# Layer 2's adjacency polynomial kept as two 64-column graphs below each other, with a new hand-written order of the steps

## The chip, the cores and the metric

The kernel runs on one core of a Trainium2 chip (trn2). The metric is the device time of one execution in microseconds; the kernel before has a median of 2142.81 us over three runs (2142.8 to 2144.53).

## The reference

128 graphs of 64 nodes with 256 features pass four graph layers in fp32; each layer is followed by a residual sum and a layer norm. What bears on this change is layer 2, and the GRU of layer 3 that the kernel runs beside it:

```python
# layer 1: normalised adjacency with self loops
adj = adj + eye(n);  d = adj.sum(-1) ** -0.5
x = layernorm(x + d[:, :, None] * adj * d[:, None, :] @ (x @ W) + b)
# layer 2: K = 4 terms of the row-normalised adjacency An = adj / (row_sum + 1e-9)
curr = h @ W.T;  out = w[0] * curr
for k in (1, 2, 3):
    curr = An @ curr;  out = out + w[k] * curr
x = layernorm(x + leaky_relu(out + b, 0.2))
# layer 3: five rounds of a GRU cell, A01 = (adj != 0)
for l in range(5):
    h = gru(A01.T @ (h @ weight[l]), h)
x = layernorm(x + h * mask)
```

The kernel does not multiply `An` three times with the features. It forms the transposed polynomial `w0 I + w1 An + w2 An^2 + w3 An^3` once for each graph (times the row sums) and gathers the features through it in one product.

## The kernel before

**Tiling.** The 128 graphs are worked on in 16 chunks of 8. A chunk's tile has 128 partitions: two graphs of 64 nodes below each other, and four such pairs side by side (`NP = 4`). A matrix of a pair, such as `Ab` or `AT1`, is a 128 x 128 block-diagonal matrix: the two 64 x 64 graphs on the diagonal and zeros beside it, zeroed once by GpSimd. `aB` holds the same adjacency dense: 128 partitions by 64 columns, two graphs below each other.

**Stages.** Layer 0 comes first (to about 325 us of the profiled span), then a loop of 79 steps for layers 1 to 3, then a tail. In a step one chunk makes one of its five GRU rounds on TensorE while the elementwise part of the other row's last round runs on VectorE, ScalarE and GpSimd. Two rows of chunks alternate, so ten steps (a block) finish two chunks; a step is named here by its number modulo ten.

**The order by hand.** In the loop the order of every engine's instructions is the order in which the program issues them, and that is the string of letters in `ORDERS`: "8", "9", "0", "1" for those steps, "p" for steps 2 to 7. A letter with a number calls one method (`step`, L1126 and on):

- `R1` to `R7` and `N1` to `N7`: the seven products of the gates r and z, and of n. An `R` has 8 matmul instructions in the trace, an `N` has 4 (each fp32 matmul counts as two). Products 1, 4, 6, 7 add up in one PSUM bank (`parz`, `pan`), 2 in another (`pbrz`, `pbn`), 5 and 3 in a third (`pdrz`, `pdn`). The pool `pg` has five banks for the six that a step takes, so a step's later `N5` starts only when an earlier bank, that of `R2`, has been read.
- `r1`, `r6`, `r7`, `n1`, `n6`, `n7`: ScalarE copies the bank (L845); the next product into it waits for that copy.
- `A2`, `A7`, `A3` and `B2`, `B7`, `B3`: VectorE adds bank and copy (L849). `R3` waits for `A7`, and `N3` waits for `B7`, which must have read the third bank. `N5` waits for `A2` in the sense above.
- `S` sigmoid, `T`/`t` tanh (ScalarE), `X` the reset gate (VectorE, L983 and L984), `U`/`u` the state update (VectorE, L946 to L948, three instructions).
- `f0`, `f1` turn the new state by VectorE and store it by a DMA, `d0`, `d1` fetch it back, `l` issues 14 loads of the next chunk, all on SP's queue, which works in order. `e` and `h` are sums on GpSimd (`Th`), `y` turns the state of a chunk that comes next.
- `G`: the messages of the next round, 16 matmuls (`pa`, L254), two ScalarE copies into `agg`, then three sums `Ta` on GpSimd (L805 to L807).
- `p`: one part of the work of layers 1 and 2 for the chunks to come, or of the output of those that are done.

**The parts.** The generator `mid` (L264) does layers 1 and 2 of a chunk in 19 parts, called M1 to M19 here; two chunks follow each other in a block, those of the second with a dash. M1: transpose `aB` into `AT1`, and `A01`. M2: row sums and their roots. M3: `dg` (diagonal of row sums), `poly3` on ScalarE, `An`. M4: add `w3 A` to it. M5: finish `AT1`. M6: first power (`power`, four matmuls, then one VectorE sum). M7: gather `ag1`. M8: bias into `xt`. M9: second power. M10, M11: products with layer 1's weights. M12: norm statistics, M13: the norm applied (four instructions, L185). M14: gather `ag2` of the normalised `xt` through the polynomial. M15 to M17: products with layer 2's weights, ScalarE, sums (L370). M18, M19: statistics and norm. The output of a chunk has four parts, O1 to O4; O4 applies a norm on ScalarE (L182).

`piece` gives the outputs' parts precedence and then goes on in `mid`. Which `p` gets which part is thereby fixed by how many stand in each string and how many of these come after `G` in step 9, where the first output is queued. In the blocks 1 to 6 of before, the first chunk's M3 is the first `p` of step 2, M13 the first of step 4, M18 the first of step 5.

Of the kernel before, what the change touches and what calls it, by code (L numbers as in the profile page):

```python
# [9 lines left out]
F32 = mybir.dt.float32  # L10
AF = mybir.ActivationFunctionType
ALU = mybir.AluOpType
# [3 lines left out]
B, N, D, HID, L = 128, 64, 256, 512, 5  # L16
# [11 lines left out]
NP = CB // 2  # L28
# [13 lines left out]
class Unit:  # L42
# [23 lines left out]

ORDERS = {
    "p": """
h u4 l u3 R1 r1 t7 R2 p u7 R5 f0 f1 e R6 r6 d0 N1 N2 A2 n1 y B2 p N6 R7 S2 X2
r7 n6 T2 p N5 R4 A7 S7 N7 n7 p B7 R3 S4 U2 N4 A3 S3 d1 X7 N3 B3 X3 X4 G p T4 T3  # L70
""",
    "8": """
h u3 u4 R1 f0 R2 p t7 l u7 r1 R5 f1 R6 N1 d0 n1 p p N2 B2 d1 N6 A2 r6 S2 X2 R7
N5 r7 R4 p A7 n6 N7 y R3 e p n7 B7 N4 A3 S4 S7 T2 X7 N3 S3 B3 X4 G X3 T4 p U2
T3
""",
    "9": """
u3 u4 R1 h R5 t7 u7 R2 r1 A2 f0 d0 R6 p f1 l N1 r6 n1 p N2 B2 S2 R7 X2 d1 p N6
r7 N5 n6 T2 R4 A7 N7 S4 e U2 n7 p R3 y B7 S7 N4 X7 G p N3 A3 S3 B3 X4 X3 T4 T3
""",  # L80
    "0": """
u3 h t7 l R1 u4 u7 R2 R5 r1 R6 f0 f1 N1 A2 r6 n1 N2 N6 R7 S2 y B2 N5 d0 p n6 r7
X2 e T2 N7 A7 p U2 d1 n7 R4 S7 p B7 R3 A3 G p N4 N3 S4 X7 S3 B3 X4 X3 T4 T3
""",
    "1": """
p h u4 R1 R2 t7 l u7 r1 u3 A2 f0 f1 R5 R6 N1 e N2 r6 n1 S2 B2 d0 p N6 n6 R7 N5
r7 A7 y N7 n7 X2 d1 T2 p p R4 B7 R3 N4 S7 U2 X7 S4 A3 N3 B3 S3 X3 G X4 p T4 T3
""",
}

# [2 lines left out]
def gnn_stack(  # L93
# [25 lines left out]
    nc = tc.nc  # L119

    wp = ctx.enter_context(tc.tile_pool(name="wp", bufs=1))
    small = ctx.enter_context(tc.tile_pool(name="small", bufs=4))
    keep = ctx.enter_context(tc.tile_pool(name="keep", bufs=1))
# [9 lines left out]
    def spread(src, n, name, pool=wp, eng=None):  # L133

        return const(bass.AP(tensor=src.tensor, offset=src.offset, ap=[[0, 128], [1, n]]), [128, n], name, eng, pool)
# [72 lines left out]
    def psum(name):  # L208
        return pt.tile([128, 512], F32, tag="pt", name=name)
# [50 lines left out]
    state = {}  # L260
    Ab = keep.tile([128, NP, 128], F32, name="Ab")
    AT1 = keep.tile([128, NP, 128], F32, name="AT1")

    def mid(c, first=False):  # L264

        aB = adjs.pop(c)
        A01 = keep.tile([128, NP, 128], F32, name="A01", bufs=4)
        with tc.issue_after(evictions[-1].ins) if first else nullcontext():
            for two in range(2):
                b = slice(two * N, (two + 1) * N)  # L270
                nc.vector.transpose(AT1[b, :, b], aB[b])
        with tc.issue_after(evictions[-1].ins) if first else nullcontext():
            nc.vector.tensor_scalar(A01, Ab, 0.0, None, op0=ALU.not_equal)
        if not first:
            yield
        rsum = small.tile([128, NP], F32, name="rsum")
        with tc.issue_after(evictions[-1].ins) if first else nullcontext():
            nc.vector.tensor_reduce(rsum, Ab, AX.X, ALU.add)
        rdeg = small.tile([128, NP], F32, name="rdeg")
        nc.vector.tensor_scalar(rdeg, rsum, 1.0, None, op0=ALU.add)  # L280
        root = inv_sqrt_begin(rdeg, NP, 128, "d1")
        rinv = small.tile([128, NP], F32, name="rinv")
        nc.vector.tensor_scalar(rinv, rsum, 1e-9, None, op0=ALU.add)
        nc.vector.reciprocal(rinv, rinv)

        nc.vector.tensor_scalar(rsum, rsum, 1e-9, None, op0=ALU.add)
        if not first:
            yield
        dg = keep.tile([128, NP, 128], F32, name="dg", bufs=1)
        nc.vector.tensor_mul(  # L290
            dg, ident[:, None, :].to_broadcast([128, NP, 128]), rsum[:, :, None].to_broadcast([128, NP, 128])
        )
        poly = keep.tile([128, NP, 128], F32, tag="poly", name="poly3", bufs=2)
        nc.scalar.activation(poly, dg, AF.Identity, scale=cw[:, 2:3])
        An = keep.tile([128, NP, 128], F32, name="An", bufs=1)
        nc.vector.tensor_mul(An, Ab, rinv[:, :, None].to_broadcast([128, NP, 128]))
        yield


        dinv1 = inv_sqrt_end(*root)  # L300
        with tc.high_priority():
            nc.vector.scalar_tensor_tensor(poly, AT1, cw[:, 3:4], poly, op0=ALU.mult, op1=ALU.add)
        if not first:
            yield
        nc.vector.tensor_add(AT1, AT1, ident[:, None, :].to_broadcast([128, NP, 128]))
        for two in range(2):
            b = slice(two * N, (two + 1) * N)
            nc.vector.tensor_mul(AT1[b, :, b], AT1[b, :, b], dinv1[b, :, None].to_broadcast([N, NP, N]))
        yield

        def power(poly, k):
            p = psum("pp").rearrange("p (q n) -> p q n", q=NP)
            for q in range(NP):
                nc.tensor.matmul(p[:, q, :], An[:, q, :], poly[:, q, :], start=True, stop=True)  # L314
            poly = keep.tile([128, NP, 128], F32, tag="poly", name=f"poly{k}", bufs=2)
            with tc.high_priority():
                nc.vector.scalar_tensor_tensor(poly, dg, cw[:, k : k + 1], p, op0=ALU.mult, op1=ALU.add)
            return poly

        def product(u, W):  # L320
            p = psum("pd").rearrange("p (q d) -> p q d", q=2)
            for h in range(2):
                q = 2 * u + h
                for k in range(2):
                    nc.tensor.matmul(  # L325
                        p[:, h, :], ag[:, k, q * 128 : (q + 1) * 128], W[:, k, :], start=k == 0, stop=k == 1
                    )
            return p

        xt = xts.pop(c)  # L330
        poly = power(poly, 1)
        if not first:
            yield
        ag = gather(halves(xt), AT1, "ag1")
        if not first:
            yield
        nc.vector.tensor_add(xt, xt, l1bs[:, None, :].to_broadcast([128, NP, D]))
        if not first:
            yield
        poly = power(poly, 0)  # L340
        yield
        for u in range(NP // 2):
            p = product(u, L1W)
            for h in range(2):
                q = 2 * u + h
                nc.vector.scalar_tensor_tensor(
                    xt[:, q, :], p[:, h, :], dinv1[:, q : q + 1], xt[:, q, :], op0=ALU.mult, op1=ALU.add
                )
            if not first:
                yield  # L350
        norm = norm_stats(xt)
        norm = norm_root(*norm)
        yield
        norm_apply(xt, *norm)
        yield


        ag = gather(halves(xt), poly, "ag2")
        yield
        for u in range(NP // 2):  # L360
            p = product(u, L2W)
            v = keep.tile([128, 2, D], F32, name="v", bufs=1)
            for h in range(2):
                q = 2 * u + h
                nc.scalar.activation(
                    v[:, h, :], p[:, h, :], AF.Prelu, bias=cb, scale=rinv[:, q : q + 1], alpha=0.2
                )
            if not first:
                yield
            nc.vector.tensor_add(xt[:, 2 * u : 2 * u + 2, :], v, xt[:, 2 * u : 2 * u + 2, :])  # L370
        if not first:
            yield
        norm = norm_stats(xt)
        norm = norm_root(*norm)
        yield
        norm_apply(xt, *norm)
        state[c] = (xt, A01)
        yield
# [12 lines left out]
    with ExitStack() as c0:  # L391
# [8 lines left out]
        loads, A, AG, HG, S2, Z, XO = {}, {}, {}, {}, {}, {}, {}  # L400
# [209 lines left out]
        p = psum0("pw")  # L610
# [3 lines left out]
        ident = const(c_ident, [128, 128], "ident", nc.scalar)  # L614
# [40 lines left out]
        for i in range(-2, NU + 1):  # L655
# [59 lines left out]
                    nc.vector.tensor_mul(gb2, b2c.rearrange("p (g k) -> p g k", k=2), gw[:, :, None].to_broadcast([128, NG, 2]))  # L715
            elif i == 1:
                with tc.issue_after(powers[-1].ins):
                    for t in (Ab, AT1):
                        nc.gpsimd.memset(t, 0.0)
                    cw = spread(conv_w, 4, "cw", eng=nc.gpsimd)  # L720
                    cb = spread(conv_b, 1, "cb", eng=nc.gpsimd)
                    l1bs = spread(l1b, D, "l1bs", eng=nc.gpsimd)
                    L1W = const_later(l1w.rearrange("(k p) e -> p k e", p=128), [128, 2, D], "L1W")
                    L2W = const_later(l2wT.rearrange("(k p) e -> p k e", p=128), [128, 2, D], "L2W")
                    bih = const_later(bihT, [128, 6], "bih")
                    bhh = const_later(bhhT, [128, 6], "bhh")
                    mask = const_later(maskT, [128, B // 2], "mask")
# [551 lines left out]
```

## Time and profile before

The profiled execution took 2143.39 us, of which 2141.6 us are its span; the granted clock of TensorE was 0.998.

| | busy, us | share of the span | instructions |
|---|---|---|---|
| TensorE matmul (PE) | 2111.7 | 99% | 10738 |
| TensorE weight load (PEld) | 1817.7 | 85% | 10738 |
| VectorE (DVE) | 1667.3 | 78% | 3849 |
| ScalarE (ACT) | 979.4 | 46% | 2006 |
| GpSimd (POOL) | 597.3 | 28% | 635 |

The busy time of TensorE is the union of its matmuls' modelled durations. These overlap: a matmul of 256 columns is shown with 379 ns, and the next one starts 216 ns after it. A gap in the stream is therefore visible only in part as idle time; the distance from start to start shows it in full. The rows that touch the polynomial (mean duration of one):

| line | what | count | ns |
|---|---|---|---|
| L271 DVE | transpose of 64 x 256, one for each half | 32 | 434 |
| L290 DVE | `dg` 128 x 512 | 16 | 768 |
| L294 ACT | `poly3` 128 x 512 | 16 | 722 |
| L302 DVE | `poly3` sum 128 x 512 | 16 | 925 |
| L305 DVE | identity added, 128 x 512 | 16 | 693 |
| L308 DVE | `AT1` scaled, 64 x 256 | 32 | 524 |
| L314 PE | power, 128 columns | 256 | 275 |
| L317 DVE | power's sum from PSUM, 128 x 512 | 32 | 742 |

### The profile page before, as it was taken

What the parts mean: (1) busy time and instruction counts of PE and PEld (TensorE: products, weight loads), DVE (VectorE), ACT (ScalarE), POOL (GpSimd) and SP (SyncE); (2) the same over time, 40 slices, a digit from 0 to 9 for tenths busy, and PEclk for the clock granted to TensorE, in tenths of its full rate; (3) what the DMA queues carried; (4) which work ended last, traced back from release to release, by engine and by line L of the source; (5) the groups of instructions that cost most, each with busy time, mean ns of one, the idle gap of its engine ahead of it and who ended that gap; (6) DMA issues with size and microseconds to landing.
All of it is one profiled execution on the core that took longest, in us unless ns stands there. A gap on an engine that the chain in (4) does not pass through costs nothing.

```text
span 2141.6 us, 31460 instructions
## 1 busy us (share of the span) xinstructions
PE 2111.7 (99%) x10738; PEld 1817.7 (85%) x10738; DVE 1667.3 (78%) x3849; ACT 979.4 (46%) x2006; POOL 597.3 (28%) x635
## 2 busy tenths in 40 slices
PE   9999999999999999999999999999999999999997
PEld 6777788888888888888888888888888888888886
DVE  3345667777888799788979898889888897888766
ACT  3333344444544455444544454444444454445444
POOL 3411131222323323222323232223232232323222
PEclk9999999999999999999999999999999999999999
DMA  6642110223421253114321342224311521234121
GB/s 166 176 134 64 37 39 21 59 55 66 95 67 40 53 110 76 43 46 87 90 52 42 76 96 63 51 62 85 81 40 47 106 74 40 60 62 96 42 59 40
DMA packets 521995, 149.77 MB, mean 70 GB/s; under 512 B 488702, under 2 KB 516860, under 8 KB 521836
## 3 DMA queue, kind: packets, MB, share of 16 engines
q1 hardware_dynamic: 516996, 142.58, 27.7%
q0 software_dynamic: 2128, 4.77, 0.9%
q8 instruction: 85, 1.39, 0.3%
q10 hardware_dynamic: 2712, 0.42, 0.1%
q14 instruction: 74, 0.61, 0.1%
HBM read 82.67 MB, written 65.01 MB: 69 GB/s over the span
## 4 chain that ended last, share of the span: by engine, by line
PE 78%; DVE 15%; issue 2%; DMA 2%; SPq 1%; ACT 1%; POOL 0%; DVEq 0%; POOLq 0%; ACTq 0%
PE parz L825 20%; PE pdrz L825 10%; PE pan L825 10%; PE pa L254 7%; PE pd L325 5%; PE pdn L825 5%; PE pbrz L825 5%; PE ps L516 5%; PE ph L500 4%; PE pbn L825 2%; DVE RZ L947 2%; DVE NI L983 1%; DVE RZ L946 1%; PE pp L314 1%; DVE NI L984 1%
## 5 line engine op out<-in xcount | busy, mean ns | idle before, releaser
L926 ACT ACTIVATE RZ<-RZ,brz 128x256 f32<-128x256 f32 x474 | 214.8, 501 | 229.3 <-DVE RZ L849 228.9
L825 PE MATMUL parz<-Th,WHH 128*128 128x256 f32 x960 | 290.8, 384 | 6.3 <-ACT c L845 6.2
L805 POOL TENSOR_TENSOR Ta<-agg 128x512 f32<-128x512 f32 x80 | 103.4, 1293 | 681.4 <-ACT agg L256 681.4
L845 ACT COPY c<-parz 128x512 f32<-128x512 f32 x240 | 138.9, 579 | 327.9 <-PE parz L825 327.3
L825 PE MATMUL parz<-Ta,V 128*128 128x256 f32 x960 | 285.5, 379 | 0.0
L825 PEld LDWEIGHTS parz<-Th,WHH 128*128 128x128 f32 x960 | 177.5, 190 | 44.8 <-ACT c L845 22.3
L825 PEld LDWEIGHTS parz<-Ta,V 128*128 128x128 f32 x960 | 182.5, 190 | 24.7
L941 ACT ACTIVATE NI<-NI,bih 128x256 f32<-128x256 f32 x316 | 151.4, 505 | 96.0 <-DVE NI L984 95.9
L845 ACT COPY c<-pan 128x512 f32<-128x512 f32 x237 | 138.1, 583 | 107.1 <-PE pan L825 106.6
L170 POOL TENSOR_TENSOR rs<-ve,mhalf 128x4 f32<-128x4 f32 (+2 forms) x65 | 66.8, 1028 | 400.5 <-DVE ve L163 347.9
L947 DVE TENSOR_TENSOR RZ<-RZ 128x256 f32<-128x256 f32 x316 | 150.4, 476 | 10.7
L805 POOL TENSOR_TENSOR Th<-hn 128x512 f32<-128x512 f32 x64 | 81.6, 1276 | 262.1 <-DVE hn L948 234.6
L849 DVE TENSOR_TENSOR NI<-pdn,c 128x512 f32<-128x512 f32 x158 | 108.3, 685 | 57.6 <-ACT c L845 50.1
L825 PE MATMUL pan<-Ta,V 128*128 128x256 f32 x474 | 144.7, 387 | 0.0
L825 PE MATMUL pan<-Th,WHH 128*128 128x256 f32 x474 | 141.0, 379 | 0.0
L946 DVE TENSOR_TENSOR RZ<-hn,NI 128x256 f32<-128x256 f32 x252 | 119.3, 474 | 23.9 <-ACT NI L941 23.5
L983 DVE SCALAR_TENSOR_TENSOR NI<-NI,bhh,RZ 128x256 f32<-128x256 f32 x237 | 121.0, 511 | 18.8 <-ACT RZ L926 10.0
L849 DVE TENSOR_TENSOR RZ<-pdrz,c 128x512 f32<-128x512 f32 x160 | 109.5, 685 | 27.6 <-ACT c L845 18.0
L254 PEld LDWEIGHTS pa<-A,h 128*128 128x128 f32 x1024 | 124.5, 192 | 7.2 <-issue 3.9
L254 PE MATMUL pa<-A,h 128*128 128x128 f32 x1024 | 125.4, 275 | 3.1 <-DMA h<-hb 2.9
L256 ACT COPY agg<-pa 128x512 f32<-128x512 f32 x160 | 92.0, 582 | 61.3 <-PE pa L254 60.5
L948 DVE TENSOR_TENSOR hn<-RZ,NI 128x256 f32<-128x256 f32 x256 | 111.2, 434 | 9.2
(225 smaller groups left out, 4782.9 us busy)
## 6 DMA issues: line engine op xcount, KB each, us to landing
hb<-flip SPq DMA_DIRECT2D x184, 256.0 KB
h<-hb SPq DMA_DIRECT2D x624, 64.0 KB
out_dram<-xt SPq DMA_DIRECT2D x30, 256.0 KB
hT<-hb SPq DMA_DIRECT2D x112, 64.0 KB
W<-in_w_dram SPq DMA_DIRECT2D x10, 512.0 KB
xt<-xb SPq DMA_DIRECT2D x32, 156.0 KB
xo<-in_x_dram SPq DMA_DIRECT2D x9, 512.0 KB
xb<-xo SPq DMA_DIRECT2D x9, 512.0 KB
```

Of the source, the lines that this page charges most:

```text
L254: nc.tensor.matmul(p[:, q * 128 : (q + 1) * 128], src(q, k), m[:, q, :], start=True, stop=True)
L325: nc.tensor.matmul(p[:, h, :], ag[:, k, q * 128 : (q + 1) * 128], W[:, k, :], start=k == 0, stop=k == 1)
L805: nc.gpsimd.tensor_sub(t[:, 0:2, :], a[:, :, H:], a[:, 0, :].rearrange("p (s n) -> p s n", s=2))
L825: nc.tensor.matmul(bank[:, g, :], w[:, q, i - 1, :], rhs, start=i in (1, 2, 5) and g == 0 and m == 0, stop=m == len(side) - 1, skip_group_ ...
L845: nc.scalar.copy(c, self.a)
L849: nc.vector.tensor_add(v, self.b if i == 2 else self.d, self.copies.pop({7: 7, 2: 1, 3: 6}[i]))
L926: nc.scalar.activation(v, self.g.a[:, q, :] if i == 4 else v, AF.Sigmoid, bias=brz[:, 2 * q + j : 2 * q + j + 1])
L941: nc.scalar.activation(n, n, AF.Tanh, bias=bih[:, 4 + j : 5 + j])
L946: nc.vector.tensor_sub(d, self.hT[:, j, f], n)
L947: nc.vector.tensor_mul(d, d, z)
L948: nc.vector.tensor_add(self.hn[:, j, f], d, n)
L983: nc.vector.scalar_tensor_tensor(n[:, j, f], h, bhh[:, 4 + j : 5 + j], r[:, j, f], op0=ALU.add, op1=ALU.mult)
```

## The change

The polynomial is kept dense. The transpose goes into a new tile `aT` (128 partitions, 64 columns for each pair) in one instruction; `dg` and `poly` have 64 columns for each pair and use `eyec`, two 64 x 64 identities below each other, loaded by two DMAs on GpSimd's queue. The first power is a product of the block-diagonal `An` (the stationary operand, as before) with 64 columns in place of 128. Only the sum of the second power goes into block-diagonal form, by one instruction for each half, in a tile `poly0` whose zeros GpSimd writes once. `AT1` gets its final values straight from `aT`.

All five strings of `ORDERS` are new as well. The matmuls of a step keep nearly their order; the `p` move, step 8 has five in place of six and step 9 six in place of five, two of them after `G`. In "p", `U2` stands ahead of the fourth `p` and `B7`. In "8", `l` comes ahead of `f0`. In "9", `A2` comes ahead of `u3`.

```diff
 "p":
-h u4 l u3 R1 r1 t7 R2 p u7 R5 f0 f1 e R6 r6 d0 N1 N2 A2 n1 y B2 p N6 R7 S2 X2
-r7 n6 T2 p N5 R4 A7 S7 N7 n7 p B7 R3 S4 U2 N4 A3 S3 d1 X7 N3 B3 X3 X4 G p T4 T3
+u3 u4 R1 r1 t7 p R2 u7 l R5 h f0 f1 e R6 r6 d0 N1 A2 n1 N2 B2 p S2 N6 R7 X2 r7
+n6 T2 p N5 R4 y A7 U2 N7 S7 n7 p S4 R3 B7 A3 N4 S3 X7 d1 N3 B3 X3 X4 G p T4 T3
 "8":
-h u3 u4 R1 f0 R2 p t7 l u7 r1 R5 f1 R6 N1 d0 n1 p p N2 B2 d1 N6 A2 r6 S2 X2 R7
-N5 r7 R4 p A7 n6 N7 y R3 e p n7 B7 N4 A3 S4 S7 T2 X7 N3 S3 B3 X4 G X3 T4 p U2
-T3
+u4 l R1 R5 R2 t7 u3 f0 u7 e r1 R6 f1 N1 h p n1 p N2 d1 A2 r6 B2 N6 S2 d0 R7 N5
+r7 X2 p n6 A7 R4 N7 p y n7 R3 B7 S4 S7 N4 A3 T2 X7 X4 N3 S3 B3 X3 U2 p T4 G T3
 "9":
-u3 u4 R1 h R5 t7 u7 R2 r1 A2 f0 d0 R6 p f1 l N1 r6 n1 p N2 B2 S2 R7 X2 d1 p N6
-r7 N5 n6 T2 R4 A7 N7 S4 e U2 n7 p R3 y B7 S7 N4 X7 G p N3 A3 S3 B3 X4 X3 T4 T3
+u4 t7 l R1 R5 p R2 r1 u7 A2 u3 f0 h d0 R6 f1 p r6 p N1 d1 n1 N2 S2 B2 X2 R7 N6
+r7 N5 n6 T2 N7 A7 U2 y R4 n7 R3 p S4 S7 e B7 N4 A3 S3 G N3 p X7 X4 B3 X3 p T4
+T3
 "0":
-u3 h t7 l R1 u4 u7 R2 R5 r1 R6 f0 f1 N1 A2 r6 n1 N2 N6 R7 S2 y B2 N5 d0 p n6 r7
-X2 e T2 N7 A7 p U2 d1 n7 R4 S7 p B7 R3 A3 G p N4 N3 S4 X7 S3 B3 X4 X3 T4 T3
+l u4 t7 u3 R1 u7 R5 f0 R2 r1 R6 f1 N1 A2 h n1 r6 N2 S2 N6 R7 n6 B2 y N5 r7 p X2
+N7 d0 T2 A7 n7 p B7 p e d1 U2 S7 R4 R3 A3 G S4 N4 p S3 N3 B3 X4 X3 T4 X7 T3
 "1":
-p h u4 R1 R2 t7 l u7 r1 u3 A2 f0 f1 R5 R6 N1 e N2 r6 n1 S2 B2 d0 p N6 n6 R7 N5
-r7 A7 y N7 n7 X2 d1 T2 p p R4 B7 R3 N4 S7 U2 X7 S4 A3 N3 B3 S3 X3 G X4 p T4 T3
+u4 p t7 u3 f0 R1 R2 u7 R5 h l r1 f1 R6 r6 N1 N2 e n1 A2 N6 d0 R7 S2 B2 n6 r7 N5
+p A7 N7 X2 n7 d1 T2 y p R4 B7 p R3 S7 A3 U2 S4 N3 B3 N4 S3 G X7 X3 X4 T4 T3 p
...
+    poly0 = keep.tile([128, NP, 128], F32, name="poly0")
...
-            for two in range(2):
-                b = slice(two * N, (two + 1) * N)
-                nc.vector.transpose(AT1[b, :, b], aB[b])
+            aT = keep.tile([128, NP, N], F32, name="aT", bufs=1)
+            nc.vector.transpose(aT, aB)
...
-        dg = keep.tile([128, NP, 128], F32, name="dg", bufs=1)
+        dg = keep.tile([128, NP, N], F32, name="dg", bufs=1)
         nc.vector.tensor_mul(
-            dg, ident[:, None, :].to_broadcast([128, NP, 128]), rsum[:, :, None].to_broadcast([128, NP, 128])
+            dg, eyec[:, None, :].to_broadcast([128, NP, N]), rsum[:, :, None].to_broadcast([128, NP, N])
         )
-        poly = keep.tile([128, NP, 128], F32, tag="poly", name="poly3", bufs=2)
+        poly = keep.tile([128, NP, N], F32, tag="poly", name="poly3", bufs=2)
...
-            nc.vector.scalar_tensor_tensor(poly, AT1, cw[:, 3:4], poly, op0=ALU.mult, op1=ALU.add)
+            nc.vector.scalar_tensor_tensor(poly, aT, cw[:, 3:4], poly, op0=ALU.mult, op1=ALU.add)
...
-        nc.vector.tensor_add(AT1, AT1, ident[:, None, :].to_broadcast([128, NP, 128]))
+        nc.vector.tensor_add(aT, aT, eyec[:, None, :].to_broadcast([128, NP, N]))
         for two in range(2):
             b = slice(two * N, (two + 1) * N)
-            nc.vector.tensor_mul(AT1[b, :, b], AT1[b, :, b], dinv1[b, :, None].to_broadcast([N, NP, N]))
+            nc.vector.tensor_mul(AT1[b, :, b], aT[b], dinv1[b, :, None].to_broadcast([N, NP, N]))
...
         def power(poly, k):
-            p = psum("pp").rearrange("p (q n) -> p q n", q=NP)
+            p = psum("pp")[:, : NP * N].rearrange("p (q n) -> p q n", q=NP)
             for q in range(NP):
                 nc.tensor.matmul(p[:, q, :], An[:, q, :], poly[:, q, :], start=True, stop=True)
-            poly = keep.tile([128, NP, 128], F32, tag="poly", name=f"poly{k}", bufs=2)
-            with tc.high_priority():
-                nc.vector.scalar_tensor_tensor(poly, dg, cw[:, k : k + 1], p, op0=ALU.mult, op1=ALU.add)
-            return poly
+            if k:
+                poly = keep.tile([128, NP, N], F32, tag="poly", name=f"poly{k}", bufs=2)
+                with tc.high_priority():
+                    nc.vector.scalar_tensor_tensor(poly, dg, cw[:, k : k + 1], p, op0=ALU.mult, op1=ALU.add)
+                return poly
+            for two in range(2):
+                b = slice(two * N, (two + 1) * N)
+                with tc.high_priority():
+                    nc.vector.scalar_tensor_tensor(
+                        poly0[b, :, b], dg[b], cw[b, 0:1], p[b], op0=ALU.mult, op1=ALU.add
+                    )
+            return poly0
...
-                    for t in (Ab, AT1):
+                    for t in (Ab, AT1, poly0):
                         nc.gpsimd.memset(t, 0.0)
+                    eyec = wp.tile([128, N], F32, name="eyec")
+                    for two in range(2):
+                        b = slice(two * N, (two + 1) * N)
+                        nc.gpsimd.dma_start(eyec[b], c_ident[b, b])
```

## The prediction

> **What bounds the kernel now.** I read the page's busy shares first, then the busy times in the ten steps of one block (780.76 to 1010.11 us), then TensorE's waits, then the timelines of the steps where it waits.
>
> ```profile
> PE 2111.7 (99%) x10738; PEld 1817.7 (85%) x10738; DVE 1667.3 (78%) x3849; ACT 979.4 (46%) x2006; POOL 597.3 (28%) x635
> ```
> TensorE is the bound. I take each matmul at its undisturbed distance to the next start, as the timeline has it (216 ns for 256 columns, 111.5 for 128, 419 for 500): together 2078 us. 54 us are gaps between matmuls: 10 in layer 0, 7 in the tail, 37 in the steps; 10 more lie before the first matmul and after the last. So only these 37 us, or cheaper matmuls, can be won.
>
> ```profile
> core 0: us, PE busy (x) PEld busy (x) DVE busy (x) ACT busy (x) POOL busy (x), PEclk, DMA share, GB/s
> 869.28:894.44 25.16, 25.16 (x134) 22.58 (x133) 18.28 (x44) 12.63 (x26) 6.56 (x7) 1.00 0.18 43
> 894.44:916.39 21.95, 20.80 (x102) 17.42 (x101) 21.17 (x50) 9.50 (x20) 7.96 (x8) 1.00 0.20 49
> 963.33:989.15 25.82, 25.82 (x134) 22.48 (x133) 20.18 (x45) 12.63 (x26) 6.45 (x7) 1.00 0.42 90
> 989.15:1010.11 20.96, 20.68 (x103) 17.52 (x102) 20.17 (x38) 9.20 (x19) 5.71 (x7) 1.00 0.35 70
> ```
> These are steps 4, 5, 8 and 9: first the length, then each engine. A step's own 84 `R`/`N` matmuls and 16 of `G` need 84 x 0.216 + 16 x 0.1115 = 19.9 us. Step 5 has no other matmuls, yet takes 21.95: VectorE is busy 21.17 of it. Step 4 is full of matmuls and VectorE has room. The bound is local: VectorE's parts pile up in steps 5 and 9.
>
> ```profile
> PE parz L825 <- ACT c L845: 6.2, 18, 1.9
> PE pdrz L825 <- DVE RZ L849: 5.1, 7, 0.8
> PE pa L254 <- DMA h<-hb: 2.9, 3, 1.3
> ```
> The second line is `R3` waiting for `A7` in step 5. By starts in the timeline, step 5 loses 0.36 at `N5`, 0.55 at `R4` and 1.06 at `R3` in each of blocks 1 to 6 (12 us in all); step 9 0.25 at `N5`, 0.55 at `R4`, 0.26 at `R5`; step 8 0.35 before and after `ag2` and 0.24 at `R7`; step 1 0.6 at `R1` and 0.45 at `R6` in three blocks; step 2 0.3 at `R1` in four.
>
> **What the Trainium skill says.** "TensorE: Matmul & The Clock Gate", section LDWEIGHTS: a weight load takes its stationary columns / 1.2, in ns, whatever the rows; 128 columns are 107 ns by it. The trace agrees, and shows what a narrower moving operand then gains:
>
> ```profile
> L484 PE MATMUL pa<-AT,xg 125*128 125x125 f32 x4 | 0.8, 286 | 0.0
> L484 PE MATMUL pa<-AT,xg 75*128 75x75 f32 x4 | 0.7, 254 | 0.0
> ...
> 269.86 0.97 PEld L484 LDWEIGHTS pa<-AT,xg 125*128 125x128 f32 x8
> 270.76 0.30 PEld L516 LDWEIGHTS ps<-W,hg 128*125 128x125 f32 x2
> ```
> Four of these eight matmuls move 125 columns, four 75 (groups by form, then the timeline of the loads). The eight loads, all of 128 columns, still run from 269.86 to 270.76: 112 ns each, the pace of the power's matmuls (8 in 0.89 us). The loads set it.
>
> "SBUF — State Buffer", section Who interferes with whom: VectorE and GpSimd share a port pair that one instruction holds as a whole; VectorE wants it for two SBUF inputs and in the two-port modes of `tensor_scalar`, not with a PSUM input. The trace agrees:
>
> ```profile
> 964.78 2.77 DVE L185 TENSOR_SCALAR xt<-xt,mv,rs 128x256 f32<-128x256 f32 x4
> ...
> 964.19 1.27 POOL L805 TENSOR_TENSOR Ta<-agg 128x512 f32<-128x512 f32 x1 [4.46 <-ACT agg L256]
> 965.54 0.73 POOL L806 TENSOR_TENSOR Ta<-agg,Ta 128x256 f32<-128x256 f32 x1
> 966.35 0.73 POOL L807 TENSOR_TENSOR Ta<-agg,Ta 128x256 f32<-128x256 f32 x1
> ...
> 965.06 0.59 PE L825 MATMUL pbrz<-hn,WHH 128*128 128x256 f32 x2
> ...
> 966.78 2.20 PE L254 MATMUL pa<-poly,xt 128*128 128x128 f32 x16
> ```
> This is M13 of the second chunk, the last `p` of step 7 in before, beside the three `Ta` sums after `G`. Alone the four take 1.3 us (1.29 at 875.68 in step 4); here 2.77, since they alternate with the sums and end at 965.61, 966.42, 967.22 and 967.55. Then `ag2` (M14), behind `R1` and `R2` of step 8, is 0.25 late: its last three pairs follow these ends by 0.06 us.
>
> **The change part by part.**
>
> *Matmuls of the power.* 256 of 64 columns. Streaming alone would be about half, 256 x 55 ns = 14 us; by the 75-column matmuls, 0. I take 0.
>
> *VectorE's work for a chunk.* M1: one transpose less, -0.44. M3: `dg` halved from 684 ns; nearest row of 128 x 256 with two SBUF inputs 425, so -0.26. M4: 745 to 480 (L983), -0.26. M5: 684 to 425, -0.26. First power: 742 to 480, -0.26. Second: two of 64 x 256, 420 to 480 each, for 742: +0.1 to +0.22. ScalarE 722 to 505. In sum -1.3 us of VectorE for each of 16 chunks, 21 us, but it counts only where VectorE is late. `poly0`'s zeros and `eyec`'s two loads stand in GpSimd's queue ahead of layer 1's weights, over 100 us before the first M1: 0, at most 1 us there. `poly0` has one buffer; its next writer comes two steps after `ag2`: 0.
>
> *The new places of the parts.* From the order of the changed program: each block from 1 on has one part more in step 9, so that all parts come one place earlier: M1 in step 0, M13 as the last `p` of step 3 (behind `X4` and `G`), M14 behind `R1` of step 4, M18 at the end of step 4, and M19, M1', M2', M3', M4' in step 5.
>
> - Step 5. Its five parts were M18 2.33, M19 1.84 (beside GpSimd), M1' 1.3, M2' 1.5, M3' 1.65: 8.6 us. Now 1.3, 0.86, 1.5, 1.1 to 1.3, 0.5: 5.4. Followed along VectorE from 895.37: M18's statistics, which need no shared port, lie where one sum (L370) took 1.75 against 0.69, so `A2` ends at 905.15 in place of 905.94. `N5` is in time, `R4` 0.13 late, `A7` ends at 909.6 and `R3` is 0.4 late. But `U2` (1.27) and M3' now precede `B7`, which ends at 912.5: `N3` 0.3 late. 0.85 lost in place of 1.97: -1.1 in 6 blocks, -6.6.
> - Step 4. M13 takes the place shown above, beside `Ta`, and `ag2` has only `R1` to cover it (1.73 less). With the same ends, `ag2` could start at 965.06 and gets its fourth pair at 967.61 where 965.73 would do: 1.9 lost, in 6 blocks +11.3. `X4` ends 1.45 us after `R1`'s start in step 8 and 1.56 in step 4, so the case is the same. Bounds: 0 if GpSimd came later, 2.7 if all four wait in full. Queued behind on TensorE: the rest of step 4.
> - Step 8. `ag2` now stands ahead of `R1`, its norm at the fourth `p` of step 7, clear of `Ta`: -0.35 x 6 = -2.1. `R7` keeps its 0.24 (ScalarE: `v`, then `r6`).
> - Step 9. M19's norm took 3.30 at 989.88 and then `u3` preceded `A2`. Now `X4` is done earlier and `u3` comes after: `A2` about 2.5 to 4 us earlier, more than `N5`'s and `R4`'s 0.8: -4.8. `R5` still waits for the first `Ta`.
> - Step 0 and 1. O4's norm on ScalarE (2.08 at 799.15) stood before `agg`'s copies; now it comes before `B7`, some 4 us earlier: `R1` -1.8, `R6` -1.4 over the three blocks. Step 2: lighter parts before it, -1.2. Block 0, step 4: M1' to M4' lighter, -0.8.
> - SP's queue. In block 0 `f1` waited behind `l` (its 14 issues from 516.74 to 523.5) and `G` 2.99 for the fetch. `l` now precedes `f0` and issues while SP is idle: -3.0. `d0`, `d1`, the stores of O4 and GpSimd's `h` move by less than the step that covers them.
>
> Sum: -6.6 - 2.1 - 4.8 - 3.2 - 1.2 - 0.8 - 3.0 = -21.7; +11.3; net -10.4. The profiled execution has 2143.4 (2141.6 and 1.8 around it), 0.6 above the median shown: 2133.0.
>
> **The rivals.**
> - *No new wait in step 4.* M13 runs ahead of `Ta`, or the norm is through first: the 21.7 stay, 2121.7. For it: VectorE may reach `X4` earlier. Against: `Ta` starts at 870.15, `X4` ends at 870.84 in step 3, 0.7 is missing.
> - *The narrow matmuls are cheaper after all:* another -14, 2119. Against it stand the loads.
> - *Given back:* half of the gains hold and the new wait eats them: 2143.4 - 10.9 + 11.3 = 2144. The tight places that I followed by hand are within 0.3 us.
> - *Slower: `B7` behind `U2` and the fourth part.* In steps 3, 5 and 7 I find `B7` 0.1 early, 0.3 late (counted), 0.45 early at `N3`. If `U2`'s three instructions meet GpSimd (830 ns against 425, so 1.2 more), `N3` is later by 1.1, 1.2 and 0.75: 3.05 x 6 = 18.3, so 2151. It decides from about 1.0 us of delay. For it: step 5 is nearly full. Against: GpSimd's sums of `Th` lie before `X2`, and VectorE idled 2.59 and 3.71 in step 3.
>
> **How the numbers follow.** 0.2% (4.3 us) is about what a measurement can tell from no change here. Forecast 2133 (own range 2127 to 2138): 0.52. No new wait 2122: 0.15. Cheaper matmuls 0.03. Given back 0.15. Slower 0.15. Faster is the first three, 0.70. The range 2120 to 2145 leaves out the slower case and a little at the low end.
>
> **What would show it.** Right: L314 still 0.89 us for eight; L317 near 480; `R3` of step 5 nearly in time; `ag2` of step 4 following L185 by 0.06 us with some 1.9 lost; no 3 us at `G` in block 0; step 9 near 20.2. Wrong: power matmuls nearer than 111 ns, waits for `B7` (L849 `NI`) in TensorE's list, or step 4 still at 25.2.

## The result and the profile after

The changed kernel has a median of 2135.23 us over five runs (2134.3 to 2135.86); the kernel before has 2142.89 us beside it over five (2142.8 to 2145.47). The ratio is 0.996, with a 95% interval of 0.9946 to 0.9974, so the change makes the kernel 0.4% faster. The profiled execution took 2135.55 us, 2133.7 of them its span; that is 7.9 us less span than before. Executions of one kernel differ in the mean clock that TensorE was granted: on one of the chips below the kernel before has a median of 2143.7 us over the six executions where it was 0.998, and 2146.5 over the five where it was 0.996, so that a ratio to the kernel before can look better than it is by up to 0.001.

The busy shares of the page after:

```profile
PE 2109.1 (99%) x10738; PEld 1819.5 (85%) x10738; DVE 1641.0 (77%) x3849; ACT 979.1 (46%) x2006; POOL 592.6 (28%) x638
```
VectorE has 26 us less to do and TensorE exactly as many instructions. The windows of steps 4, 5, 8 and 9, one block of after (length, then busy time of each engine):

```profile
core 0: us, PE busy (x) PEld busy (x) DVE busy (x) ACT busy (x) POOL busy (x), PEclk, DMA share, GB/s
863.87:891.00 27.13, 26.05 (x135) 22.71 (x134) 18.01 (x35) 12.68 (x26) 5.45 (x6) 1.00 0.16 40
891.00:911.51 20.51, 20.51 (x102) 17.41 (x101) 19.72 (x52) 10.21 (x21) 7.57 (x8) 1.00 0.21 52
960.24:983.93 23.69, 23.69 (x119) 20.62 (x117) 16.46 (x37) 11.48 (x25) 5.80 (x7) 1.00 0.31 65
983.93:1004.20 20.27, 20.27 (x102) 17.57 (x101) 19.59 (x39) 10.08 (x21) 6.06 (x6) 1.00 0.36 72
```
Step 4 grew from 25.16 to 27.13 and TensorE is idle 1.08 us in it. Step 5 shrank from 21.95 to 20.51, step 9 from 20.96 to 20.3. Step 8 is not to be compared alone: a gather of 16 matmuls that stood in it before now stands in step 7. Steps 6, 7 and 8 together went from 72.8 to 72.4.

TensorE's waits after (in total, times, longest):

```profile
engine line waited for: us in total, times, longest us
PE pa L254 <- DVE xt L185: 6.4, 18, 0.4
PE parz L837 <- ACT c L857: 2.9, 3, 2.2
...
PE pdrz L837 <- DVE RZ L861: 0.2, 1, 0.2
```
`R3`'s wait for `A7` (the line with `pdrz`, 5.1 us before) has become 0.2, and the wait for ScalarE's copies has fallen from 6.2 to 2.9, of which 2.2 lie in the tail. The first line is new: a gather that waits for the norm, 18 times, which is three waits in each of six blocks.

### The profile page after: what moved, and what is told of

It is laid out like the page before. It is cut to its first block, busy times and chain, and to the rows that moved or that the text cites. A ratio compares the mean times of both kernels' runs of the same rounds, so it can differ in the third digit from the quotient of the medians.

```text
span 2133.7 us, 31438 instructions
## 1 busy us (share of the span) xinstructions
PE 2109.1 (99%) x10738; PEld 1819.5 (85%) x10738; DVE 1641.0 (77%) x3849; ACT 979.1 (46%) x2006; POOL 592.6 (28%) x638
## 4 chain that ended last, share of the span: by engine, by line
PE 91%; DVE 6%; DMA 1%; issue 1%; POOL 0%; ACT 0%; SPq 0%; POOLq 0%; DVEq 0%; ACTq 0%
PE parz L837 24%; PE pdrz L837 12%; PE pan L837 12%; PE pa L254 9%; PE pbrz L837 6%; PE pdn L837 6%; PE pd L333 5%; PE ps L524 5%; PE ph L508 4%; PE pbn L837 3%; PE pa L492 1%; PE pp L314 1%; PE po L546 1%; DVE xt L185 1%; PE pf L644 1%; DVE NI L996 1%
## 5 line engine op out<-in xcount | busy, mean ns | idle before, releaser
L837 PEld LDWEIGHTS parz<-Th,WHH 128*128 128x128 f32 x960 | 178.9, 190 | 35.6 <-ACT c L857 10.4
L959 DVE TENSOR_TENSOR RZ<-RZ 128x256 f32<-128x256 f32 x316 | 161.1, 510 | 10.8
L958 DVE TENSOR_TENSOR RZ<-hn,NI 128x256 f32<-128x256 f32 x252 | 115.6, 459 | 27.8 <-ACT NI L953 27.2
```

Of the source, the lines that this page charges most:

```text
L837: nc.tensor.matmul(bank[:, g, :], w[:, q, i - 1, :], rhs, start=i in (1, 2, 5) and g == 0 and m == 0, stop=m == len(side) - 1, skip_group_ ...
L958: nc.vector.tensor_sub(d, self.hT[:, j, f], n)
L959: nc.vector.tensor_mul(d, d, z)
```

## The experiments

The runs below were made on two chips. One had the first two experiments on step 4, the dense form alone and the order alone, and the kernel before has a median of 2145.42 us there over 16 executions; the other had the remaining four, with 2145.31 over 25. That is some 2.5 us more than beside the result, and every ratio is to the kernel before on the same chip. Beside the ratios I set the spans of the profiled executions, all with a mean clock of 0.997 to 0.999: 2141.6 us for the kernel before and 2133.7 for after. "Lost" means here, as in the prediction, the distance from one matmul's start to the next beyond the undisturbed distance.

My theory was the prediction's: the lighter VectorE work and the new places of the parts win some 20 us, and one new wait in step 4, made by the port that VectorE and GpSimd share, takes half of it back. The rivals: the wait there has another cause; the order alone, or the dense form alone, does it all; or the matmuls got cheaper.

**The wait of step 4: its place.** The step where the new wait arises, in the timeline of after (start, length, engine, line, operation):

```profile
864.73 1.27 POOL L817 TENSOR_TENSOR Ta<-agg 128x512 f32<-128x512 f32 x1 [3.20 <-ACT agg L256]
...
864.90 3.18 DVE L185 TENSOR_SCALAR xt<-xt,mv,rs 128x256 f32<-128x256 f32 x4
...
866.07 0.73 POOL L818 TENSOR_TENSOR Ta<-agg,Ta 128x256 f32<-128x256 f32 x1
...
866.20 0.49 PE L254 MATMUL pa<-poly,xt 128*128 128x128 f32 x2 [0.44 <-DVE xt L185]
...
866.88 0.72 POOL L819 TENSOR_TENSOR Ta<-agg,Ta 128x256 f32<-128x256 f32 x1
...
867.01 0.49 PE L254 MATMUL pa<-poly,xt 128*128 128x128 f32 x2 [0.32 <-DVE xt L185]
...
867.81 1.71 PE L254 MATMUL pa<-poly,xt 128*128 128x128 f32 x12 [0.32 <-DVE xt L185]
```
M13's four instructions take 3.18 us here. The three waiting starts of the gather, 866.20, 867.01 and 867.81, come 0.20 us after the ends of GpSimd's three sums (866.00, 866.80, 867.60): a norm instruction is through only when a sum lets it. 1.97 us are lost, and the same in each of the blocks 1 to 6. The first experiment gives the gather the cover of one more product:

```diff
-u3 u4 R1 r1 t7 p R2 u7 l R5 h f0 f1 e R6 r6 d0 N1 A2 n1 N2 B2 p S2 N6 R7 X2 r7
+u3 u4 R1 r1 t7 R2 p u7 l R5 h f0 f1 e R6 r6 d0 N1 A2 n1 N2 B2 p S2 N6 R7 X2 r7
```

> The changed kernel with one edit: in the string of steps 2 to 7 the first p stands behind R2 in place of R1. Only TensorE's order changes; VectorE, ScalarE, GpSimd and SP keep theirs. Theory (ag2 of step 4 waits for a norm that is late beside Ta): R2 covers 1.73 of the 1.97 us in blocks 1 to 6, so step 4 goes from 27.13 to about 25.4 us and the whole from 2135.2 to about 2125. Rival (the wait only moves on, to R5 or later in step 4 or 5): step 4 shorter, step 5 longer by as much, 2134 to 2136.

It took 2125.48 us (2124.68 to 2126.17), ratio 0.9907 (0.9893 to 0.9921). The gather of step 4 loses 0.25 in place of 1.97, and step 5 is as it was, down to its 0.25 at `R3` and 0.20 at `N3`. The span of 2123.6 us is 10.1 under after's: the wait did cost its full 10 us, and nothing behind it in the steps 4 and 5 took its place. (In this execution `R3` of step 0 also lost 1.6 more than in after and the tail 1.3 less; both differ from execution to execution, as said below.)

**The wait of step 4: its cause.** This kernel leaves TensorE's, VectorE's and ScalarE's orders as they are. Only GpSimd gets one small instruction more, two columns of a copy, that needs M13's result and stands ahead of the first `Ta` sum of the steps 3 (blocks 1 to 6). `later` and `behind` put the sums after M13:

```diff
-            self.ta = sums(self.agg, "a")
+            if not later:
+                self.ta = sums(self.agg, "a")
...
+                for t in behind:
+                    guard = small.tile([128, 2], F32, name="guard")
+                    nc.gpsimd.tensor_copy(guard, t[:, 2:4, D - 1])
+                    w.ta = sums(w.agg, "a")
+                behind = []
...
-                    w.messages()
+                    if s > 10 and s % (2 * L) == 3 and s < 70:
+                        behind = [xts_now[0]]
+                        w.messages(True)
+                    else:
+                        w.messages()
```

> The changed kernel, with GpSimd's three sums Ta of step 3 (blocks 1 to 6) put behind a two-column copy on GpSimd that reads the result of M13, so that M13 has the shared port for itself. VectorE's and TensorE's orders are untouched; six small copies are added. Theory (M13 is late because it alternates with Ta): its four instructions end within 1.3 to 1.4 us, ag2 loses about 0.5 us in place of 1.97, 2135.2 to about 2126.5. Rival (M13 is late because VectorE reaches it late, the port matters little): step 4 stays at 27.1, 2135, or worse if the later Ta holds up R5.

It took 2124.33 us (2123.12 to 2126.03), ratio 0.9901 (0.9886 to 0.9917). Its timeline at the same place:

```profile
862.97 1.37 DVE L185 TENSOR_SCALAR xt<-xt,mv,rs 128x256 f32<-128x256 f32 x4
...
863.66 2.12 PE L254 MATMUL pa<-poly,xt 128*128 128x128 f32 x16
...
864.40 0.32 POOL L1166 COPY guard<-xt 128x2 f32<-128x2 f32 x1 [4.81 <-DVE xt L185]
864.67 1.27 POOL L818 TENSOR_TENSOR Ta<-agg 128x512 f32<-128x512 f32 x1
864.71 1.52 DVE L961 TENSOR_TENSOR RZ<-RZ 128x256 f32<-128x256 f32 x1
```
The same four norm instructions at the same place in VectorE's stream take 1.37 us when GpSimd is silent, and the sixteen matmuls run nearly in one piece, 0.17 lost where about 0.5 was expected. So it is GpSimd's sums that made M13 slow, as the Trainium skill has it ("SBUF — State Buffer", section Who interferes with whom). The price has only moved: the second instruction of a state update (L961) now stands beside the sum and takes 1.52 us, against 0.43 in after. Nothing waits for it so closely, and no time is lost there.

**Both together,** the two edits above in one kernel:

> The changed kernel with both of the earlier repairs: GpSimd's first `Ta` sum of the steps 3 held back until M13's norm is through, and the first `p` of string p behind `R2` in place of `R1`. If both take away the same wait (port), the gains don't add: the 0.17 or 0.25 that each left in step 4 of six blocks goes, 1 to 1.5 us below either alone, about 2123. If they were two separate gains of 10 us each, about 2114.

It took 2124.03 us (2123.23 to 2125.34), ratio 0.9905 (0.9891 to 0.9918). Step 4 is back at 25.16 without any loss. The median is 0.3 and 1.5 us below those of the single edits, and the ranges overlap; two separate gains of 10 us would have given about 2114. By the profiled spans it is 2121.4 us against 2123.2 with the guard alone: 1.0 is the six times 0.17 that the guard had left, 1.2 a tail that differs from execution to execution (below), and step 0 lost 0.4 more. The two edits remove one wait, not two.

**The dense polynomial without the new order.** After's code with the five strings of before:

```diff
 "p":
-u3 u4 R1 r1 t7 p R2 u7 l R5 h f0 f1 e R6 r6 d0 N1 A2 n1 N2 B2 p S2 N6 R7 X2 r7
+h u4 l u3 R1 r1 t7 R2 p u7 R5 f0 f1 e R6 r6 d0 N1 N2 A2 n1 y B2 p N6 R7 S2 X2
...
```

> The dense polynomial alone: the changed kernel with the five strings of the kernel before. Theory (the dense form is worth something only where VectorE is late, the rest is the order's): R3 of step 5 is 0.4 to 0.5 us earlier in blocks 1 to 6 and block 0 gains 0.5, so 2139 to 2140, with no new wait in step 4 (25.16). Rival (the dense form carries the gain, the order little): 2135 or below. Rival (no gain without the order): 2142 to 2143.

It took 2137.87 us (2137.69 to 2139.33), ratio 0.9967 (0.9954 to 0.9979). That is a larger gain than expected, and by the ratio alone it can't be told from the 0.996 (0.9946 to 0.9974) of the whole change. The spans do part them: 2135.9 us here, 2133.7 for after.

**The new order without the dense polynomial.** Before's code with the five strings of after:

> The new order alone: the kernel before, with block-diagonal polynomial, and the five new strings. Theory: the wait of 1.97 in step 4 is there too, since it is the order's; in step 5 M1' and M3' are 0.7 us longer ahead of B7, so R3 and N3 lose about 1.1 in place of 0.45 per block; steps 1, 8, 9 and block 0's G gain as in the changed kernel: 2139 to 2140. Rival (the order alone carries all): 2135 to 2136. Rival (without the lighter parts the new order is a loss): 2143 and above.

It took 2140.99 us (2140.01 to 2143.72), ratio 0.9982 (0.9974 to 0.999). Step 5, in the windows of the kernel with the dense form alone and then of the one with the order alone:

```profile
893.35:914.73 21.38, 20.79 (x102) 17.41 (x101) 20.63 (x49) 9.50 (x20) 7.97 (x8) 1.00 0.21 50
```
```profile
865.29:892.42 27.13, 26.06 (x134) 22.71 (x133) 18.01 (x35) 12.67 (x26) 5.45 (x6) 1.00 0.16 40
892.42:913.51 21.09, 20.61 (x102) 17.41 (x101) 20.27 (x53) 10.43 (x21) 7.58 (x8) 1.00 0.21 51
```
Step 5 takes 21.95 before, 21.38 with the dense form, 21.09 with the order and 20.51 with both. The two gains, 0.57 and 0.86, add up to the 1.44 of after: both relieve VectorE in the same step, and it was late by more than either gives. Over all 79 steps the dense form alone is 5.7 us shorter than before, the order alone 3.1 (its wait in step 4 counted) and both 9.6, so the rival that one of them does it all falls, although the dense form has the larger part of the net. The first line of the second fence is step 4: its 27.13 us, and 1.97 lost at the gather, are there without the dense form too, while the dense form alone leaves step 4 at 25.16. The wait of step 4 therefore belongs to the new order alone. The other waits go the same way: the dense form alone leaves the 3.35 us at block 0's `G` and the waits at `R1` and `R6` of step 1 (2.6 us); the order alone removes the first and leaves 1.2 us at `R6`.

**The loads ahead of the stores.** In after, with `l` put back behind `f0` in string "8":

```diff
-u4 l R1 R5 R2 t7 u3 f0 u7 e r1 R6 f1 N1 h p n1 p N2 d1 A2 r6 B2 N6 S2 d0 R7 N5
+u4 R1 R5 R2 t7 u3 f0 l u7 e r1 R6 f1 N1 h p n1 p N2 d1 A2 r6 B2 N6 S2 d0 R7 N5
```

> The changed kernel with one letter moved: in string 8 the 14 loads of `l` come behind `f0` again, as in the kernel before. Theory of SP's queue: in block 0 the fetch for `G` of step 8 waits behind the loads again and about 3.0 us come back there, once, so about 2138.2 in all. Rival: it was the whole new order that took the wait away, and `l` alone changes nothing (2135.2).

It took 2143.3 us (2142.13 to 2145.32), ratio 0.9992 (0.9983 to 1.0): the place was right and the price too low. Block 0 loses 6.7 us at `G`, 5.0 of them waiting, and the blocks 1 to 5 another 0.2 to 1.06 each, 3.3 in all; 2.8 come back in step 9, step 0 and the tail. SP's queue in block 0 of this kernel (start, time that the issues took), and below it in after:

```profile
515.46 1.26 SPq L224 DMA_DIRECT2D Ab<-in_adj_dram  x2
516.77 3.92 SPq L229 DMA_DIRECT2D aB<-in_adj_dram  x8
...
522.29 0.38 SPq L980 DMA_DIRECT2D hb<-flip  x1
527.02 3.75 SPq L988 DMA_DIRECT2D h<-hb  x8
```
```profile
507.28 0.34 SPq L239 DMA_DIRECT2D xt<-xb  x1
515.07 2.35 SPq L980 DMA_DIRECT2D hb<-flip  x2
519.66 3.77 SPq L988 DMA_DIRECT2D h<-hb  x8
```
The store of `f1` goes out at 522.29, behind the loads; in after both stores are out at 517.42. Then nothing is issued for 4.35 us, and the fetches of both halves follow. In the kernel before, the queue went on with a fetch at 524.05, right behind its store of 523.57, because there `d0` stands ahead of `d1` and needs only the earlier store. In the new string `d1` comes first, needs the store just issued, and holds `d0` back. That this makes a wait of 5.0 out of 3.0 fits the queue; it was not tried by itself. The other 1.7 of the 6.7 us are no wait. This is the gather behind it, and below it the same gather in after:

```profile
532.51 3.75 PE L254 MATMUL pa<-A,h 128*128 128x128 f32 x16 [4.88 <-DMA h<-hb]
```
```profile
527.49 1.95 PE L254 MATMUL pa<-A,h 128*128 128x128 f32 x16
```
Its sixteen matmuls start 0.213 us from each other, in after 0.112: the granted clock of TensorE was 0.51 from 530.2 to 537.1, where it is 1.00 in after. The `R1` behind them loses 0.6 more by that. What brings such a stretch on was not tried.

**The narrow matmuls.** In after, the power's matmuls issued twice into the same bank (the second pass writes the same values):

```diff
-            for q in range(NP):
-                nc.tensor.matmul(p[:, q, :], An[:, q, :], poly[:, q, :], start=True, stop=True)
+            for _ in range(2):
+                for q in range(NP):
+                    nc.tensor.matmul(p[:, q, :], An[:, q, :], poly[:, q, :], start=True, stop=True)
```

> The changed kernel with the power's 64-column matmuls issued twice into the same bank: 256 matmul instructions more, half of them in step 1 and the others where M6 and M9 stand. If the loads of 128 columns set the pace, each costs 0.1115 us: 28.5 us more, about 2163.7. If the streamed columns set it, each costs about 0.055: 14.3 more, about 2149.5. If they vanish in waits that are there anyway, under 10 more.

It took 2162.88 us (2162.41 to 2163.75), ratio 1.0085 (1.0072 to 1.0099). That is 27.8 us more span than after. One power and the product behind it, in the timeline of after and of this kernel:

```profile
828.23 1.00 PE L314 MATMUL pp<-poly,An 128*128 128x64 f32 x8
...
829.07 0.65 PE L837 MATMUL pdn<-Ta,V 128*128 128x256 f32 x2
```
```profile
838.81 1.90 PE L315 MATMUL pp<-poly,An 128*128 128x64 f32 x16
...
840.54 0.65 PE L838 MATMUL pdn<-Ta,V 128*128 128x256 f32 x2
```
From start to start eight take 0.84 us and sixteen 1.73: 0.89 for eight more, 111 ns each. The kernel before took 0.89 for its eight of 128 columns; the 0.05 that after lacks is made up by the matmul behind it, so that in both kernels the rest follows 0.89 us after the first. Half the columns cost the same as all of them.

**Whose work the gains of step 1 are.** In after, the string "0" of before:

```diff
-l u4 t7 u3 R1 u7 R5 f0 R2 r1 R6 f1 N1 A2 h n1 r6 N2 S2 N6 R7 n6 B2 y N5 r7 p X2
-N7 d0 T2 A7 n7 p B7 p e d1 U2 S7 R4 R3 A3 G S4 N4 p S3 N3 B3 X4 X3 T4 X7 T3
+u3 h t7 l R1 u4 u7 R2 R5 r1 R6 f0 f1 N1 A2 r6 n1 N2 N6 R7 S2 y B2 N5 d0 p n6 r7
+X2 e T2 N7 A7 p U2 d1 n7 R4 S7 p B7 R3 A3 G p N4 N3 S4 X7 S3 B3 X4 X3 T4 T3
```

> The changed kernel with the string 0 of the kernel before. If that string's new order makes the new losses of step 0 (R3 0.78, R6 0.73, N6 0.13 over the blocks, about 1.8 us), they go: about 2133.5, unless what they cover moves into step 1. If they come from the lighter VectorE parts and the earlier `p` of step 9, they stay: 2135.2. If the gains of step 1 (4.1 us at R1 and R6) came from this string, they are lost again: about 2139.

It took 2144.22 us (2142.15 to 2147.05), ratio 0.9996 (0.9988 to 1.0004). The third case holds for `R6` of step 1 alone, and the loss there is larger than what had been won: 8.3 us, 1.1 to 1.5 in each of the blocks 2 to 7. `R1` and `G` of step 1 lose nothing here either. The first case falls: of the new losses of step 0 only the 0.4 at `N6` goes, while `R6` loses 0.9 and `R3` 2.8, which is 2.0 more than in after. The chain that leads to `R6`, in the timeline of block 3:

```profile
1021.90 2.08 ACT L182 ACTIVATE xt<-xt,nb,rs 128x256 f32<-128x256 f32 x4 [0.55 <-DVE nb L1089]
1023.88 0.57 ACT L857 COPY c<-pan 128x512 f32<-128x512 f32 x1
...
1024.48 0.69 DVE L861 TENSOR_TENSOR NI<-pdn,c 128x512 f32<-128x512 f32 x1 [0.70 <-ACT c L857]
...
1025.68 2.15 DVE L1081 SCALAR_TENSOR_TENSOR xt<-h,mask,xt 128x128 f32<-128x128 f32 x4
...
1031.96 0.91 ACT L953 ACTIVATE NI<-NI,bih 128x256 f32<-128x256 f32 x2 [0.34 <-DVE NI L996]
1032.78 0.56 ACT L857 COPY c<-parz 128x512 f32<-128x512 f32 x1
1033.39 0.70 PE L837 MATMUL parz<-Th,WHH 128*128 128x256 f32 x2 [1.24 <-ACT c L857]
```
O4's norm on ScalarE (L182) stands ahead of `n7`'s copy, so VectorE's `B7` waits for it. The next part of the output, on VectorE (L1081), then meets the `Ta` sums and takes 2.15 us for 1.13; the reset gates come late, the tanh instructions come late on ScalarE, and the copy of `r1`, behind them in ScalarE's order, holds up `R6`. In after, the norm runs at 1019.36, behind the copy of `pan` at 1018.71, and `R6` of the next step loses nothing.

That `R1` and `G` of step 1 keep their gain fits the place of the norm: in block 2 it starts 18.4 us after the first matmul of step 0 in before and 18.3 with the dense form alone, 14.5 in after, and 15.5 here, so that `agg`'s copies, which start at 20.4 and 20.8 in before, are in time at 18.8 and 19.2. String "0" is the old one here, so it is the other new strings that move the norm; that it is the one `p` more in step 9 was argued and not tried by itself.

## Why the prediction was right

The mechanisms were those forecast, and the net of 10.4 us came out as 7.9 by the profiled spans. That it is so near is in part luck: the gains in the steps come to 21.5 us for 21.7, but the steps 1, 2 and 5 gave 3.6 more than forecast and the steps 0, 6 to 8 and 9 took 3.8 away. Measured terms against the forecast ones:

| term | forecast, us | measured, us |
|---|---|---|
| step 4, new wait at the gather | +11.3 | +11.8 |
| step 5 | -6.6 | -8.6 |
| step 8 (steps 6 to 8 together, without block 0's `G`) | -2.1 | -1.8 |
| step 9 | -4.8 | -3.1 |
| step 1 | -3.2 | -4.2 |
| step 0 | (with step 1) | +1.8 |
| step 2 | -1.2 | -1.8 |
| block 0, step 4 and `G` | -3.8 | -3.8 |
| layer 0 and tail | 0 | about +1.7 |

- *Matmuls of the power, 0.* Right, and shown by the doubled matmuls. The Trainium skill's price of a load ("TensorE: Matmul & The Clock Gate", section LDWEIGHTS; 107 ns for 128 columns) is near the 111 ns measured. The rival of cheaper matmuls falls.
- *Step 4.* The mechanism, the place and the size held: 1.97 each against 1.9. The experiments that give cover or move the sums come down to 0 to 0.25, the lower bound. The rival without this wait was put at 2121.7; the three kernels that remove it took 2124.0 to 2125.5. So nearly all of the gains were there, and the wait stood against them.
- *Step 5.* The loss was put at 0.85 and is 0.53: `R3` 0.25 for 0.4, `N3` 0.20 for 0.3, `R4` 0.08 for 0.13. The stream that I followed by hand was 0.05 to 0.15 us too pessimistic at each. The step with the dense form alone and the one with the order alone show that both halves of the argument, lighter work and other parts, were needed.
- *Step 9.* This term was mis-sized. What was named did go: `N5` and `R4` lose nothing any more, 4.8 us. But `N7` now loses 0.13 in every block and `R3` 0.2 to 0.3 in three, which gave 1.6 back. I had followed the old waits to their end and not looked for new ones in the order that replaced them.
- *Step 0 and step 1.* The gain at `R1` (1.8), `R6` (1.4) and at a DMA for `G` (1.0) in step 1 was 4.2; the DMA I had not counted. O4's norm does come some 4 us earlier, and `agg`'s copies with it, as argued. String "0" is needed for `R6` alone, by a way that I had not seen: without it the earlier norm stands before `n7`'s copy and so before `B7`. Step 0 itself gave 1.8 back, at `R6` (0.73, in one block), `R3` (0.78) and `N6` (0.4 over before), where I had counted nothing. `R3` there differs from execution to execution, between 0.59 and 2.39 among the kernels with this string; what it depends on stays open.
- *SP's queue.* Right: the 3 us at `G` of block 0 are gone, and moving `l` alone brings back a wait of 5.0.
- *Tail.* It lost 7.4 us in this execution against 5.8 before (the prediction had 7). Of the seven experiments with after's last steps, five lost 6.1 there and two 7.3 like after, without an edit near it. What parts them is the clock: in after and in these two the granted clock was 0.5 for 3.41 us (in after from 2103.83), and seven matmuls in a row start 0.427 us from each other in place of 0.216. That costs 1.7 us, of which a later wait gives 0.3 back; the other five and before have no such stretch there. So these 1.3 us are a difference between executions and no effect of the change. The remaining 0.3 are in every kernel with the new strings: one product waits 2.3 us for ScalarE's copy where before has 2.0. Layer 0 ended at the same time to within 0.05 us.
- *Slower, by `B7` behind `U2` and the fourth part.* It did not happen. `N3`, which waits for `B7`, loses 0.20 in step 5 and at most 0.03 in the steps 3 and 7.

The kernel that keeps the whole change and moves one letter (2125.48) or holds GpSimd back (2124.33) is faster than both: 0.9% under before, where the change as made is 0.4% under it.

## What to carry to other kernels

Where a part is moved one place earlier, look at what runs on the other engine that shares its port at the new place, and count how much cover the consumer keeps there: here one letter decided 10 us, more than the whole change brought. Narrowing the moving side of the power's matmuls brought nothing, since the load of their 128 stationary columns takes longer (111 ns) than 64 columns would at the pace of 256 in 216 ns (an estimate of 54 ns), but the lighter elementwise work on the narrow result paid where VectorE was the late engine. And a place where a wait disappears should be followed on through the new order, since a third or more of such a gain (1.6 of 4.8 in step 9, 1.8 of 4.2 in steps 0 and 1) was taken by smaller waits that had not been there before.

## What was not expected of the hardware

An instruction added to GpSimd, with a wait, made the kernel 10.5 us faster by the profiled spans (2133.7 to 2123.2), by starting GpSimd's sums 1.9 us later in the step, when the norm was through. Four norm instructions beside three sums took 3.18 us and alone 1.37, so that the overlap cost VectorE 1.8 us. One update instruction that met the long sum took 1.52 us for 0.43. GpSimd's sums themselves took nearly the same with and without that overlap: 1.27 and 0.73 us for the first two beside the norm, 1.27 and 0.79 in the kernel that holds them back, where they meet a state update. And the clock of TensorE was granted at half for a stretch of 3.41 us in the tail of some executions and not of others with the same instructions, and for 6.83 us that began in TensorE's wait of 5.0 us for the late fetch.
